# Selective scan in a two-layer block: carried states copied by ScalarE in every batch; in the first batch, two directions added to y by TensorE and a quarter of GpSimd's C products made by VectorE

## The chip, the cores and the metric

The kernel runs on one core of one Trainium2 chip. Its engines work on instruction streams of their own, each in order, and wait for each other by semaphores: TensorE (PE, with its weight loads as PEld), VectorE (DVE), ScalarE (ACT), GpSimd (POOL) and SyncE (SP), which issues most of the DMAs. The metric is the device time of one execution in microseconds. Before the change it is 4207.36 us, the median of three runs (4205.96 to 4208.89).

## The reference, cut to what matters

The input x has shape (4, 384, 32, 32), all in float32. Two layers follow each other, each with a mixer and a feed-forward part; the change lies in the first layer's mixer, a selective scan over the image in four directions:

```python
xs = _cross_scan(x)      # rows, columns, and both of these backwards: (B, 4, 384, 1024)
x_dbl = jnp.einsum('bkdl,kcd->bkcl', xs, x_proj_weight)
dts, Bs, Cs = (x_dbl[:, :, :R], x_dbl[:, :, R:R + N], x_dbl[:, :, R + N:])
dt = jax.nn.softplus(einsum(dts, dt_projs_weight) + dt_projs_bias)
def step(h, inp):        # over the 1024 positions, with 16 states n per channel d
    dA = jnp.exp(dtt[..., None] * A)
    h = h * dA + (dtt * ut)[..., None] * bt[:, :, None, :]
    y = jnp.einsum('bkdn,bkn->bkd', h, ct)
ys = ys + Ds * u         # then the four directions are turned back and added to y
```

After it come a layer norm with GELU and a residual, an expert layer (two of four experts per token), and in the second layer an attention with 8 heads and a factored feed-forward.

## The kernel before, in words

**Stages.** `scan_layer` runs the scan of the four batches one after the other. When a batch's scan is done, `between` puts the rest of the work of the batch before it (routing, experts, attention, feed-forward) into the program, so that the tail of batch b runs beside the scan of batch b + 1. The tail of the last batch stands alone at the end.

**The scan's units.** A unit is (batch, direction k, half i of the sequence), 512 positions long; the directions come in `ORDER = (0, 1, 3, 2)`, so k = 2 is the last. A unit has three chunks of 128 channels (`chunk`), and a chunk four state groups g of four states. In a group, partitions hold 4 states x 32 channels, and the chunk's 128 channels are four blocks j of 32, in two pairs q. For each pair:

- POOL multiplies `dtr` (dt times u, spread over the states by DMA) by the B rows `bcs` into `bx`, 128x1024 (L445);
- ACT makes `da`, the exponential of dt times A, into PSUM, 128x512 for each block (L454); `da` has two buffers;
- DVE scans each block (L459). In pair 0 the states go into `bx` in SBUF, in pair 1 into `da` in PSUM. In the first half of a sequence the scan starts from zero, in the second half from `carry`;
- in pair 1, DVE copies the last column of the state into `carry` in the first half (L465), and multiplies the state by the C rows into `bx` (L466);
- in pair 0, DVE copies two last columns in the first half (L470), and POOL multiplies both blocks of `bx` by the C rows, 128x1024 (L473);
- PE sums over the states with `sel`, into the chunk's `acc` in PSUM (L480).

`bx` has six buffers; `acc` shares two banks of PSUM with the other products of the scan (`dt_ps`, `xd_ps`, the layer norms). After a chunk, DVE adds `acc` into `y`: with D times u at k = 0 (L291), else L295. For k = 1 and 3, `y` is read and written by columns of the image. `project` makes dt, dt times u and the B and C rows of the next unit while a unit runs. In batch 0 its softplus is summed by PE with identity products (L383) and needs no POOL; in the other batches POOL and DVE do it (L400, L401, L407).

**What sets the order.** The program is written in the order above, but a scheduler that simulates a timeline puts the instructions of each engine into the order in which they then stand in that engine's stream. `place_behind` asks that parts of `project` stand behind the current group's POOL and DVE products. On the chip each stream is in order: an instruction that waits holds everything behind it on its engine.

Of the kernel before, what the change touches and what calls it, by code (L numbers as in the profile page):

```python
# [17 lines left out]
P = 128  # L18
# [5 lines left out]
HF = 512  # L24
# [3 lines left out]
ORDER = (0, 1, 3, 2)  # L28
# [30 lines left out]
NG = NS // NJ  # L59
# [54 lines left out]
def halves(i):  # L114
    return slice(i * HF, (i + 1) * HF)


class Body:
# [69 lines left out]
    def scan_layer(self, x1, between):  # L188

        nc, tc, a = self.nc, self.tc, self.a  # L190
        with ExitStack() as ctx:
# [23 lines left out]
            def start(b):  # L215
                x = work.tile([P, DC, L], F32, tag="u", name="u")
                src = a["x"][b].rearrange("(c p) l -> p c l", p=P)
                if b > 0:
                    nc.sync.dma_start(out=x, in_=src)
                    self.layernorm(x, x, self.eps6, psum, work)  # L220
                    return x

                for i in range(NH):
                    nc.sync.dma_start(out=x[:, :, halves(i)], in_=src[:, :, halves(i)])
                self.layernorm(x, x, self.eps6, psum, work, parts=[0])
                return x

            def finish(b, y, i):

                self.layernorm(y, y, self.eps5, psum, work, parts=[i])  # L230
                for c in range(DC):
                    ins = nc.scalar.activation(
                        y[:, c, halves(i)], y[:, c, halves(i)], AF.Gelu,
                        bias=self.col("lnb", c), scale=self.col("lnw", c),
                    ).ins
                    rows = slice(c * P, (c + 1) * P)
                    x = work.tile([P, HF], F32, tag="k2", name="x", bufs=6)
                    nc.sync.dma_start(out=x, in_=a["x"][b][rows, halves(i)])
                    nc.gpsimd.tensor_add(x, x, y[:, c, halves(i)])
                    if i == 0 and b < B - 1:  # L240
                        self.fresh.setdefault(b, []).append(x)
                    else:
                        nc.sync.dma_start(out=x1[b][rows, halves(i)], in_=x)
                self.exp_again(ins)
# [17 lines left out]
            carry = None  # L262
            for n, unit in enumerate(units):
                b, k, i = unit
                fed, ahead = ahead, []
                project = iter(())
                if n + 1 < len(units):
                    nb = units[n + 1][0]
                    if nb not in us:
                        us[nb] = start(nb)  # L270
                    project = self.project(units[n + 1], us[nb], wx, work, dram, psum, ahead)
                    next(project)
                if n % NH == 0:
                    carry = wp.tile([P, NB * NG], F32, tag=f"carry{n // NH % 2}", name="carry")
                if k == 0 and i == 0:
                    y = work.tile([P, DC, L], F32, tag="y", name="y")
                for c in range(DC):
                    acc = psum.tile([P, HF], F32, tag="ps", name="acc")
                    for _ in self.chunk(
                        unit, n % NH == 0, c, fed, carry, nega, sel, acc, work, dap  # L280
                    ):
                        next(project, None)
                    if k % 2 == 0:
                        ys = y[:, c, halves(i)]
                        out = acc
                    else:
                        w = slice(i * (HW // NH), (i + 1) * (HW // NH))
                        ys = y[:, c, :].rearrange("p (h w) -> p h w", h=HW)[:, :, w]
                        out = acc.rearrange("p (w h) -> p h w", h=HW)
                    if k == 0:  # L290
                        nc.vector.scalar_tensor_tensor(  # L291
                            ys, us[b][:, c, halves(i)], dsum[:, c : c + 1], out, op0=ALU.mult, op1=ALU.add
                        )
                    else:
                        nc.vector.tensor_add(ys, ys, out)  # L295
                if k == ORDER[-1]:
                    self.under_way.setdefault(b, fed[2])
                    finish(b, y, i)
                    if n + 1 == len(units) or units[n + 1][0] != b:
                        between(b)  # L300
# [113 lines left out]
    def chunk(self, unit, first, c, fed, carry, nega, sel, acc, work, dap):  # L414

        nc = self.nc
        b, k, i = unit
        bcs, dd, _ = fed  # L420
        dtr = []
        for q in range(NJ // 2):

            pair = []
            at = c * P + q * 2 * DB
            for s in range(2):
                t = work.tile([P, 2, HF], F32, tag="dtr", name="dtr", bufs=7)
                for n in range(NJ):
                    nc.sync.dma_start(
                        out=t[n * DB : (n + 1) * DB],  # L430
                        in_=dd[s, at : at + 2 * DB, :].rearrange("(j d) l -> d j l", d=DB),
                    )
                pair.append(t)
            dtr.append(pair)

        def run(ap):
            return ap[:, ::-1] if k >= 2 else ap

        last = 0 if k >= 2 else HF - 1
        for g in range(NG):  # L440
            bc = bcs[g]
            out = []
            for q in range(NJ // 2):
                bx = work.tile([P, 2, HF], F32, tag="bx", name="bx", bufs=6)
                pool = nc.gpsimd.tensor_mul(  # L445
                    bx, dtr[q][1], bc[:, 0].unsqueeze(1).to_broadcast([P, 2, HF])
                ).ins
                cg = bc[:, 1]
                at = ((c * 2 + q) * NG + g) * 2
                for j in range(2):  # L450
                    block = c * NJ + 2 * q + j
                    col = (k * NB + block) * NG + g
                    da = dap.tile([P, HF], F32, tag="da", name="da")
                    nc.scalar.activation(  # L454
                        da, dtr[q][0][:, j, :], AF.Exp, scale=nega[:, col : col + 1]
                    )
                    hold = carry[:, at + j : at + j + 1]
                    h = bx[:, j, :] if q == 0 else da
                    nc.vector.tensor_tensor_scan(  # L459
                        run(h), run(da), run(bx[:, j, :]), 0.0 if first else hold,  # L460
                        ALU.mult, ALU.add,
                    )
                    if q == 1:
                        if first:
                            nc.vector.tensor_copy(hold, h[:, last : last + 1])  # L465
                        dve = nc.vector.tensor_mul(bx[:, j, :], h, cg).ins  # L466
                if q == 0:
                    if first:
                        for j in range(2):
                            nc.vector.tensor_copy(  # L470
                                carry[:, at + j : at + j + 1], bx[:, j, last : last + 1]
                            )
                    pool = nc.gpsimd.tensor_mul(  # L473
                        bx, bx, cg.unsqueeze(1).to_broadcast([P, 2, HF])
                    ).ins
                out.append(bx)
            for q in range(NJ // 2):
                for j in range(2):
                    lo = (2 * q + j) * DB
                    nc.tensor.matmul(  # L480
                        acc[lo : lo + DB, :], sel, out[q][:, j, :],
                        start=(g == 0), stop=(g == NG - 1),
                    )
            self.place_behind = {"pool": pool, "dve": dve}
            yield
# [1087 lines left out]
```

## Time and profile before

| | before |
|---|---|
| median of three runs | 4207.36 us |
| the profiled execution | 4218.98 us, span 4217.2 us |
| scan of batch 0 (first to last scan instruction) | 44.0 to 748.6 us |
| scan of batches 1, 2, 3 | 751.9 to 1641.7, 1650.8 to 2541.5, 2542.2 to 3423.0 us |
| busy: PE, DVE, ACT, POOL | 3343.3, 2870.7, 2505.8, 3020.9 us |
| L445, POOL | 768 times 2359 ns |
| L473, POOL | 384 times 2360 ns |
| L459, DVE | 1536 scans of 1210 to 1273 ns |
| L466, DVE | 768 times 679 ns |
| L465 and L470, DVE | 384 times 149 ns and 384 times 142 ns |
| L454, ACT | 1536 times 690 ns |
| L295, DVE | 72 times 678 ns |

How to read it: the profile is one execution, taken by the hardware's profiler. A line such as "L473 POOL TENSOR_TENSOR bx<-bx,bcs" is a group of instructions by source line, engine, operation, and names of what is written and read. In a timeline, a line has the start, the time taken, the engine, the line, and in brackets how long the engine had been idle and what ended that. In the page's slices each digit is the busy share of one fortieth of the span, in tenths. A program's float32 product on PE shows as two matmul records.

### The profile page before, as it was taken

The numbers are of one execution on the slowest core, as the hardware profiler recorded it, in microseconds if no ns is written. First come the engines' busy times: TensorE is split into PE (matmuls) and PEld (weight loads), VectorE is DVE, ScalarE is ACT, GpSimd is POOL, SyncE is SP. The second block draws the span as 40 slices with busy tenths as digits, with TensorE's granted clock in tenths as the row PEclk, the third lists the DMA queues.
The fourth block names the chain that finished last, engine by engine and source line by source line (L and its number), as shares of the span: only waits on it lengthen the run. The fifth ranks groups of instructions, "written<-read, shape, count | busy, mean of one in ns | idle before, by whom it ended". The sixth has DMA issues, their size and how long they took to land. (4 is left out here: it accounts for less than half of the span.)

```text
span 4217.2 us, 45878 instructions
## 1 busy us (share of the span) xinstructions
PE 3343.3 (79%) x13372; PEld 1576.0 (37%) x13372; DVE 2870.7 (68%) x4250; ACT 2505.8 (59%) x4510; POOL 3020.9 (72%) x1476
## 2 busy tenths in 40 slices
PE   6445544389987888699987888789986898999899
PEld 2111111155653223255553223246553234676333
DVE  5999997878887777788877877788887851100101
ACT  5555555466665776766665775766665763533353
POOL 5999997888989877889989976988989941000100
PEclk9666666589998999799998998789998999999999
DMA  5454464577886444578886434578886424446200
GB/s 144 126 130 124 124 172 107 163 221 219 250 245 171 110 121 126 169 227 227 238 245 184 125 94 133 163 212 228 243 252 188 109 71 154 129 169 217 64 6 31
DMA packets 378882, 677.65 MB, mean 161 GB/s; under 512 B 49920, under 2 KB 179328, under 8 KB 378624
## 3 DMA queue, kind: packets, MB, share of 16 engines
q1 hardware_dynamic: 368800, 647.42, 54.0%
q0 software_dynamic: 8192, 25.21, 2.0%
q8 instruction: 107, 1.75, 0.2%
q10 hardware_dynamic: 1632, 2.04, 0.2%
q14 instruction: 151, 1.24, 0.1%
HBM read 566.68 MB, written 107.79 MB: 160 GB/s over the span
## 5 line engine op out<-in xcount | busy, mean ns | idle before, releaser
L445 POOL TENSOR_TENSOR bx<-dtr,bcs 128x1024 f32<-128x1024 f32 x768 | 1792.6, 2359 | 181.7 <-PE acc L480 99.5
L454 ACT ACTIVATE da<-dtr,nega 128x512 f32<-128x512 f32 x1536 | 1044.7, 690 | 920.4 <-DVE bx L466 568.7
L473 POOL TENSOR_TENSOR bx<-bx,bcs 128x1024 f32<-128x1024 f32 x384 | 904.5, 2360 | 139.7 <-DVE carry L470 68.2
L480 PE MATMUL acc<-bx,sel 128*32 128x512 f32 x3072 | 491.0, 700 | 322.5 <-POOL bx L473 296.2
L990 PE MATMUL h_ps<-xc,w 128*128 128x256 f32 (+1 forms) x3168 | 652.1, 361 | 55.4 <-DMA w<-in_w 31.7
L1011 PE MATMUL y_ps<-w,hs 128*128 128x384 f32 x1824 | 634.9, 501 | 34.2 <-ACT hs L1003 23.0
L990 PEld LDWEIGHTS h_ps<-xc,w 128*128 128x128 f32 x3168 | 546.2, 195 | 210.5 <-issue 94.6
L459 DVE TENSOR_TENSOR_SCAN bx<-da,carry,bx 128x512 f32<-128x512 f32 x384 | 474.0, 1269 | 116.3 <-POOL bx L445 61.2
L459 DVE TENSOR_TENSOR_SCAN da<-da,carry,bx 128x512 f32<-128x512 f32 x384 | 475.8, 1273 | 74.5 <-ACT da L454 67.1
L459 DVE TENSOR_TENSOR_SCAN bx<-da,bx 128x512 f32<-128x512 f32 x384 | 451.8, 1210 | 98.4 <-POOL bx L445 55.7
L466 DVE TENSOR_TENSOR bx<-da,bcs 128x512 f32<-128x512 f32 x768 | 509.0, 679 | 3.9 <-DMA bcs<-both 0.4
L459 DVE TENSOR_TENSOR_SCAN da<-da,bx 128x512 f32<-128x512 f32 x384 | 455.2, 1218 | 69.0 <-ACT da L454 55.8
L1011 PEld LDWEIGHTS y_ps<-w,hs 128*128 128x128 f32 x1824 | 348.7, 195 | 317.9 <-issue 60.8
L1144 PE MATMUL s_ps<-w 64*128 64x512 f32 x1024 | 310.3, 663 | 75.4 <-ACT ex L1150 71.4
L1150 ACT ACTIVATE ex<-s_ps 128x512 f32<-128x512 f32 x512 | 300.5, 591 | 107.6 <-PE s_ps L1144 106.2
L1042 POOL DMA_INDIRECT got<-made,g_source x64 | 61.0, 954 | 422.4 <-DMA made<-y 402.7
L998 ACT ACTIVATE hs<-h_ps,bb 128x256 f32<-128x256 f32 (+1 forms) x528 | 200.0, 440 | 230.2 <-PE h_ps L990 229.8
L1193 PE MATMUL o_acc<-ex,vt 128*64 128x512 f32 x1024 | 286.9, 637 | 24.4 <-ACT ex L1150 21.0
L480 PEld LDWEIGHTS acc<-bx,sel 128*32 128x32 f32 x3072 | 73.4, 115 | 610.5 <-POOL bx L473 403.1
L1015 DVE TENSOR_TENSOR y<-y_ps,bb 128x384 f32<-128x384 f32 x76 | 41.7, 548 | 255.9 <-PE y_ps L1011 255.9
L1144 PEld LDWEIGHTS s_ps<-w 64*128 64x128 f32 x1024 | 83.6, 191 | 285.4 <-ACT ex L1150 238.1
L370 PE MATMUL dt_ps<-xd,wdt 108*128 108x512 f32 x192 | 121.9, 721 | 58.8 <-ACT mag L409 29.3
(240 smaller groups left out, 3630.4 us busy)
## 6 DMA issues: line engine op xcount, KB each, us to landing
w<-in_w SPq DMA_DIRECT2D x352, 576.0 KB
dtr<-dd SPq DMA_DIRECT2D x1536, 128.0 KB
bcs<-both SPq DMA_DIRECT2D x512, 128.0 KB
dd<-one_e SPq DMA_DIRECT2D x96, 256.0 KB
dd<-mag SPq DMA_DIRECT2D x96, 256.0 KB
xt<-x SPq DMA_DIRECT2D x32, 384.0 KB
made<-y SPq DMA_DIRECT2D x32, 384.0 KB
xs<-rows SPq DMA_DIRECT2D x28, 385.0 KB
```

What stands on the lines that cost most here:

```text
L445: pool = nc.gpsimd.tensor_mul(bx, dtr[q][1], bc[:, 0].unsqueeze(1).to_broadcast([P, 2, HF])).ins
L454: nc.scalar.activation(da, dtr[q][0][:, j, :], AF.Exp, scale=nega[:, col : col + 1])
L459: nc.vector.tensor_tensor_scan(run(h), run(da), run(bx[:, j, :]), 0.0 if first else hold, ALU.mult, ALU.add,)
L466: dve = nc.vector.tensor_mul(bx[:, j, :], h, cg).ins
L473: pool = nc.gpsimd.tensor_mul(bx, bx, cg.unsqueeze(1).to_broadcast([P, 2, HF])).ins
L480: nc.tensor.matmul(acc[lo : lo + DB, :], sel, out[q][:, j, :], start=(g == 0), stop=(g == NG - 1),)
L990: ins = nc.tensor.matmul(ps[:, r, :], w1[(f + r) // wf][:, c, (f + r) % wf * P : ((f + r) % wf + 1) * P], xc[:, c, :], start=(c == 0), sto ...
L998: done = nc.scalar.activation(hs[:, f + r, :], ps[:, r, :], AF.Gelu if last else AF.Identity, bias=bb[:, f + r : f + r + 1],).ins
L1011: nc.tensor.matmul(out[:, :D], hs[:, f, t * P : (t + 1) * P], w2[f // wf][:, f % wf, :], start=(f == 0), stop=(f == FC - 1),)
L1144: ins = nc.tensor.matmul(ps, w[rows, j * P : (j + 1) * P], w[rows, halves(i)], start=True, stop=True).ins
L1150: done.append(nc.scalar.activation(ex[:, o, :], ps, AF.Exp, scale=HD**-0.5, accum_out=sums[:, t, 2 * j + o, i : i + 1],).ins)
L1193: ins = nc.tensor.matmul(out[cols, :], made[t][1][:, j, cols], ex[:, o, :], start=(j == 0), stop=(j == MB - 1),).ins
```

## The change

Three edits, all in the scan:

- The last column of a state goes into `carry` by a ScalarE copy instead of a VectorE copy, in every batch. For pair 0, one copy of two columns takes the place of two copies of one.
- In batch 0, for the directions 1 and 3, PE adds the chunk's part of `y` to `acc` by a product with the identity, which ends the accumulation, and ACT copies `acc` into `y`. Before, DVE added.
- In batch 0, in the groups 1 and 3, POOL multiplies one block of pair 0 by the C rows, 128x512, and DVE the other.

```diff
+                    if b == 0 and k not in (0, ORDER[-1]):
+                        nc.tensor.matmul(out, self.ident, ys, start=False, stop=True)
+                        nc.scalar.copy(ys, out)
-                    if k == 0:
+                    elif k == 0:
                         nc.vector.scalar_tensor_tensor(
                             ys, us[b][:, c, halves(i)], dsum[:, c : c + 1], out, op0=ALU.mult, op1=ALU.add
                         )
...
                     if q == 1:
                         if first:
-                            nc.vector.tensor_copy(hold, h[:, last : last + 1])
+                            nc.scalar.copy(hold, h[:, last : last + 1])
                         dve = nc.vector.tensor_mul(bx[:, j, :], h, cg).ins
                 if q == 0:
                     if first:
-                        for j in range(2):
-                            nc.vector.tensor_copy(
-                                carry[:, at + j : at + j + 1], bx[:, j, last : last + 1]
-                            )
-                    pool = nc.gpsimd.tensor_mul(
-                        bx, bx, cg.unsqueeze(1).to_broadcast([P, 2, HF])
-                    ).ins
+                        nc.scalar.copy(carry[:, at : at + 2], bx[:, :, last])
+                    if b == 0 and g % 2 == 1:
+                        pool = nc.gpsimd.tensor_mul(bx[:, 0, :], bx[:, 0, :], cg).ins
+                        nc.vector.tensor_mul(bx[:, 1, :], bx[:, 1, :], cg)
+                    else:
+                        pool = nc.gpsimd.tensor_mul(
+                            bx, bx, cg.unsqueeze(1).to_broadcast([P, 2, HF])
+                        ).ins
...
                         acc[lo : lo + DB, :], sel, out[q][:, j, :],
-                        start=(g == 0), stop=(g == NG - 1),
+                        start=(g == 0),
+                        stop=(g == NG - 1 and not (b == 0 and k not in (0, ORDER[-1]))),
```

## The prediction

> **What bounds the kernel now.** I read the page first (slices, groups), then the sums by stretch, then the timeline of the first batch, then single lines. In the chain that ended last, nothing of the scan stands: it is the last batch's attention and FFN on TensorE, the same instructions in both kernels. The change is therefore worth what it does to the stretch before that, the scan, which ends at about 3424 us. The slices on the page (about 105 us each) and the stretches:
>
> ```profile
> DVE  5999997878887777788877877788887851100101
> POOL 5999997888989877889989976988989941000100
> PEclk9666666589998999799998998789998999999999
> ...
> 133.70:634.20 500.50, 243.59 (x766) 59.43 (x766) 462.87 (x612) 266.81 (x416) 498.13 (x217) 0.65 0.53 134
> 634.20:751.90 117.70, 55.19 (x165) 18.08 (x165) 91.52 (x112) 62.33 (x97) 94.45 (x46) 0.63 0.43 114
> 751.90:1641.70 889.80, 723.84 (x3043) 356.88 (x3044) 711.04 (x1032) 579.45 (x1071) 768.93 (x376) 0.90 0.65 183
> ```
>
> The columns of the last three are the stretch, its length, busy time of PE, PE's weight loads, DVE, ACT and POOL, and the granted clock. The first is six half-sequences of batch 0: POOL is busy 498 of 500 us and DVE 463, while ACT and PE are about half idle. The third is batch 1, with the first batch's experts and attention beside the scan: nothing is full there (PE 81%, POOL 86%, DVE 80%, ACT 65%). So batch 0 is bound by POOL with DVE close behind, and batches 1 to 3 by the way the engines wait for each other. One state group of batch 0 in the timeline, DVE and then POOL:
>
> ```profile
> 308.47 2.46 DVE L459 TENSOR_TENSOR_SCAN bx<-da,carry,bx 128x512 f32<-128x512 f32 x2 [0.23 <-ACT da L454]
> 310.85 2.44 DVE L459 TENSOR_TENSOR_SCAN da<-da,carry,bx 128x512 f32<-128x512 f32 x2
> 313.20 1.26 DVE L466 TENSOR_TENSOR bx<-da,bcs 128x512 f32<-128x512 f32 x2
> 314.70 2.46 DVE L459 TENSOR_TENSOR_SCAN bx<-da,carry,bx 128x512 f32<-128x512 f32 x2 [0.23 <-ACT da L454]
> ...
> 311.05 4.64 POOL L445 TENSOR_TENSOR bx<-dtr,bcs 128x1024 f32<-128x1024 f32 x2
> 315.66 2.33 POOL L473 TENSOR_TENSOR bx<-bx,bcs 128x1024 f32<-128x1024 f32 x1
> 317.96 4.66 POOL L445 TENSOR_TENSOR bx<-dtr,bcs 128x1024 f32<-128x1024 f32 x2
> ```
>
> Starts, not durations, are what to read, since instructions of an engine overlap by 0.05 to 0.1 us. POOL goes round in 317.96 - 311.05 = 6.91 us; DVE could in 314.70 - 308.47 = 6.23 us, its 0.23 us wait for ACT within. Per chunk (four groups) POOL needs 27.7 us; measured are 500.5 / 18 = 27.8. DVE needs 4 x 6.23, the y add (0.60) and the product with u (0.83), 26.35 us. **The slack of DVE behind POOL is 1.4 us a chunk**; whatever is moved from POOL to DVE has to fit in it.
>
> **The change part by part.**
>
> *Carry copies (all batches).* DVE loses 384 copies at L465 and 384 at L470; ACT gets 384 and 192 (two columns in one). Their durations (149 and 142 ns) overstate what leaves DVE: in the timeline a copy of L465 moves the next start by 0.05 to 0.06 us, a pair of L470 by 0.20. The first half-sequence of each direction (the second has none) holds 24 and 12 of these, 24 x 0.055 + 12 x 0.20 = 3.7 us, or 1.2 a chunk. On ACT the nearest row is the 128x2 copy at L691, 0.18 us; 36 copies are 6.5 us a half-sequence. In ACT's order they stand between the exps: the copy from `bx` just ahead of the fourth exp of a group, the two from `da` ahead of the next group's first. Behind them wait the exps (and the scans on them), the dt chain, and in batches 1 to 3 the expert evictions L998 and the GELUs; POOL's C product now waits for ACT instead of DVE.
>
> *y adds of two directions (batch 0).* Twelve DVE adds (0.60 us) leave; PE gets twelve identity products (1.6 us each by the L383 rows, two passes of about 0.8), ACT twelve copies (0.585, row L409). PE is 49% and ACT 53% busy in batch 0, and the product stands behind the chunk's last sums, so I cost these at nothing; without that cover it is 12 x 2.2 = 26 us. DVE gains 0.3 a chunk over all.
>
> *A quarter of the C products (batch 0).* In 48 groups POOL's product halves: 2.31 becomes 1.22 (start to start of the 128x512 subtraction L400), 2.2 us less a chunk, 52 us in all. DVE gets 48 products of 0.60 us by L466. But L466 reads `da` in PSUM and one operand in SBUF; the new product reads `bx` and the C rows, both in SBUF, and no scan instruction of before does that. What such an instruction costs beside POOL, the few DVE lines with two SBUF inputs, and one with a tensor and a scalar column, show:
>
> ```profile
> 1607.48 1.55 DVE L1228 TENSOR_TENSOR wc<-wc,cols 128x384 f32<-128x384 f32 x1
> 2561.86 0.54 DVE L1228 TENSOR_TENSOR wc<-wc,cols 128x384 f32<-128x384 f32 x1
> ...
> 1607.36 1.26 POOL L400 TENSOR_TENSOR mag<-one_e,mag 128x512 f32<-128x512 f32 x1
> 1608.58 2.67 POOL L473 TENSOR_TENSOR bx<-bx,bcs 128x1024 f32<-128x1024 f32 x1
> ...
> 1250.85 1.27 DVE L970 TENSOR_TENSOR apart<-xs,full_i 128x8 f32<-128x8 f32 x1 [3.03 <-DMA xs<-rows]
> ...
> 2548.88 9.57 DVE L1223 TENSOR_SCALAR wb<-wb,c2mean 128x384 f32<-128x384 f32 x1 [4.17 <-DMA wb<-in_wb]
> ...
> 2548.95 9.28 POOL L445 TENSOR_TENSOR bx<-dtr,bcs 128x1024 f32<-128x1024 f32 x4
> ```
>
> The same product takes 0.54 us with POOL idle and 1.55 while POOL works: it ended 0.4 us after the POOL instruction that was running, and POOL's next took 2.67 instead of 2.36. L970 took 1.27 and 0.27 beside POOL against 0.17 without. So DVE waits for the running POOL instruction: 1.0, 1.1 and 0.1 us, mean 0.73; POOL loses up to 0.31. The L1223 row, another kind, waited through four POOL instructions.
>
> The Trainium skill (SBUF — State Buffer, Who interferes with whom) says this against the change: a VectorE instruction with two SBUF inputs takes a read port that GpSimd needs too, and the later of the two blocks until the first has finished. By that rule a product that meets a 2.3 us instruction at a random moment would wait an estimated 1.15 us, 55 us for 48. The rows here say 0.73, or 35 us; the 9.57 row shows more than the one instruction that the page allows.
>
> *Batch 0, sum.* POOL: 27.7 - 2.2 + 2 x 0.31 = 26.1 us a chunk; it is no longer the bound. DVE, bare: 26.35 + 2 x 0.60 - 0.3 (y) - 0.6 (copies, 1.2 in every second half-sequence) = 26.65, or 24 x (26.65 - 27.8) = -28 us: the low end. With 2 x 0.73 of port waits it is 28.1. DVE also waited, between 100 and 630 us, 8.8 us for the second pair's exps and 4.2 for the dt product, 0.7 a chunk, which POOL's pace hid and DVE's does not; part of it falls together with the port waits, so I take half: 28.45, **+16 us**. High end: 2 x 1.1 and all of the 0.7, 29.55, +42 us. What is late next is DVE; POOL will idle at its C products.
>
> *Batches 1 to 3, sum.* Twelve first half-sequences: 12 x 3.7 = 44 us leave DVE, 12 x 6.5 = 78 us come to ACT. Both wait for each other there: between 752 and 3424 us ACT waits 584 us for DVE before its exps, DVE 190 us for these exps. With ACT's waits the larger I take three quarters of the copies as hidden (+20) and count 0.35 of what DVE loses (-15): **+5 us**, between -30 (two thirds of DVE's share, copies hidden) and +50 (two thirds of ACT's on the path).
>
> *Rest.* No DMA is added or taken away. By the built program's order the experts and attention stand beside the same chunks as before, mostly within a twelfth of a half-sequence (the latest, attention of batch 1, a quarter later), so I give the order nothing. Sum: +21 us. The profiled execution took 4219.0 us (span 4217.2 and 1.8 around it), 11.6 above the median of 4207.4; it would go to 4240, the median to 4228.
>
> **The rivals.**
>
> *Faster: the products meet POOL while it waits.* If DVE is the bound, POOL runs ahead and stands idle at its half product, which needs the same scan as DVE's half; DVE then starts first and waits for nothing. For it: the two halves are ready together. Against it: after a C product POOL has two L445 (4.6 us) and arrives at the next about when DVE does. It gives -28 us in batch 0, and with 0 to -5 beyond about 4177. It decides if the wait per product is under 0.2 to 0.4 us: bare DVE is 1.15 a chunk below now, less the 0.35 to 0.7 of other waits, for two products.
>
> *Slower still, by ScalarE.* The copies wait in order for scans, and evictions and GELUs (L1003, 2.77 us with two table loads of 1.28) behind them start late. For it: DVE's largest wait in batches 1 to 3 is for ACT (112 us for the second pair). +50 there with +16 in batch 0 give 4273.
>
> *No difference.* POOL's 52 us leave the bound and the port waits eat just that: about 4207. Here too belongs that a stage does what the change says (POOL falls to some 94%) and the end does not move.
>
> **How the numbers follow.** A measurement here can tell about 0.2%, 8.4 us, from no change. Forecast (port waits of about 0.7): 0.46, its own range 4212 to 4255. ScalarE on the path: 0.12. No difference: 0.14. Faster: 0.28. Slower is 0.46 + 0.12 = 0.58. The range goes from 4172 (the faster case and 5 us) to 4275 (the ScalarE case, or waits of 1.1 with some +20 beyond); below and above it I leave 0.08 each.
>
> **What would show it.** Right: the new VectorE product has a mean well above 0.68 us, near 1.4, and those over 1 us end just behind a POOL instruction; POOL is under 97% busy in batch 0 and waits for DVE's scans at the C products; a chunk of batch 0 takes 28 us or more. Right for ScalarE: the small copies take about 0.18 us and the exps after them start no later. Wrong: the product's mean is 0.7 and a chunk takes 27 us or less (faster), or batches 1 to 3 (890, 900 and 882 us now) change by more than 15 us each, which nothing in my sum carries.

## The result, and the profile after

The changed kernel takes 4285.21 us (median of five runs, 4277.44 to 4289.87), the kernel before took 4208.89 us beside it (4205.96 to 4214.97). The ratio is 1.0175, with an interval of 1.0159 to 1.0191: slower by some 76 us. The forecast was 4228 us, with a range up to 4275. The direction was right, the size less than a third of what came, and the time lies outside the range.

The profiled execution after took 4289.86 us, with a span of 4288.0 us: 70.8 us more span than before. Read by the first and last scan instruction of each batch, these divide as follows.

| stretch | before | after | difference | forecast |
|---|---|---|---|---|
| first scan of batch 0 to first scan of batch 1 | 707.9 | 746.8 | +38.9 | +16 |
| from there to the last scan of batch 3 | 2671.1 | 2692.1 | +21.0 | +5 |
| from there to the end | 794.2 | 804.8 | +10.6 | 0 |

So half of the loss lies in batch 0, and nearly half behind it. The slices of the page after, in the rows that were shown of before:

```profile
DVE  6999998867887877687877877686887851000101
...
POOL 5988887888897978788988967888998941000100
PEclk8777766579998999789998999789998999999999
```

Of the five slices at 9 that POOL had at the start, one is left; DVE keeps its five. The stretches of the profile after (length, then busy time of PE, weight loads, DVE, ACT, POOL, and the granted clock). The first line is the whole of batch 0, the next two are its half-sequences 1 to 6 and the last one, the fourth is batch 1, the fifth batches 1 to 3:

```profile
44.30:791.10 746.80, 404.42 (x1099) 106.26 (x1097) 678.07 (x700) 398.24 (x743) 644.78 (x298) 0.72 0.48 124
...
137.10:675.10 538.00, 295.78 (x792) 73.55 (x791) 495.63 (x492) 283.76 (x536) 475.82 (x218) 0.72 0.50 127
675.10:791.10 116.00, 54.27 (x160) 17.68 (x157) 97.59 (x118) 62.55 (x96) 88.28 (x45) 0.63 0.39 106
791.10:1691.40 900.30, 723.74 (x3054) 356.65 (x3055) 703.68 (x841) 591.38 (x1215) 768.19 (x375) 0.90 0.64 182
...
791.10:3483.20 2692.10, 2233.43 (x9291) 1092.50 (x9291) 2104.18 (x2555) 1814.01 (x3612) 2301.34 (x1123) 0.91 0.64 182
```

And the whole of batch 0, and batches 1 to 3, in the kernel before:

```profile
44.00:751.90 707.90, 350.57 (x1076) 92.29 (x1074) 635.53 (x856) 377.30 (x588) 674.67 (x297) 0.67 0.51 131
...
751.90:3423.00 2671.10, 2234.18 (x9299) 1091.74 (x9299) 2135.26 (x3130) 1776.22 (x3185) 2303.10 (x1124) 0.91 0.65 184
```

Busy time and idle time are what to take from these. In batch 0 DVE's busy time grew from 635.5 to 678.1 us, by 42.6; its idle time went from 72.4 to 68.7 us, by -3.7. The two make the 38.9. POOL is busy 30 us less and idle 102 us where it was idle 33. So POOL did get its relief, and DVE got nothing for it: it waits as long as before, and works longer. In batches 1 to 3 the granted clock is 0.91 in both kernels and PE's busy time the same within 0.8 us (2234.2 and 2233.4), so a slower TensorE is not what lengthens them.

What the new instructions cost (groups of the profile after: busy time, mean ns of one, then the engine's idle time ahead and what ended it):

```profile
L477 POOL TENSOR_TENSOR bx<-bx,bcs 128x1024 f32<-128x1024 f32 x336 | 793.8, 2366 | 194.1 <-ACT carry L472 95.4 <-DVE bx L462 92.7 <-DMA bcs<-both 3.7
...
L469 DVE TENSOR_TENSOR bx<-da,bcs 128x512 f32<-128x512 f32 x768 | 497.8, 677 | 48.8 <-ACT carry L468 45.5 <-DMA dtr<-dd 0.3
...
L475 DVE TENSOR_TENSOR bx<-bx,bcs 128x512 f32<-128x512 f32 x48 | 68.6, 1429 | 5.4 <-ACT carry L472 4.7
L474 POOL TENSOR_TENSOR bx<-bx,bcs 128x512 f32<-128x512 f32 x48 | 68.2, 1420 | 17.8 <-ACT carry L472 12.2 <-DVE bx L462 5.6
```

L475 is the new VectorE product, with 1.43 us in the mean where the product from PSUM (L469) takes 0.68. L469 stands here for another reason, which was not foreseen: it now waits 45.5 us for ScalarE's copy of the carry. Both read the same tile `da`, and the built program makes the second reader wait for the first.

A stretch of batch 0 in the timeline after, DVE and then POOL (start, time taken, and in brackets the wait before):

```profile
321.35 2.46 DVE L462 TENSOR_TENSOR_SCAN bx<-da,carry,bx 128x512 f32<-128x512 f32 x2 [1.31 <-POOL bx L448]
323.85 2.63 DVE L475 TENSOR_TENSOR bx<-bx,bcs 128x512 f32<-128x512 f32 x1
326.40 2.45 DVE L462 TENSOR_TENSOR_SCAN da<-da,carry,bx 128x512 f32<-128x512 f32 x2
...
338.98 0.69 DVE L475 TENSOR_TENSOR bx<-bx,bcs 128x512 f32<-128x512 f32 x1
...
316.65 2.34 POOL L477 TENSOR_TENSOR bx<-bx,bcs 128x1024 f32<-128x1024 f32 x1 [0.53 <-DVE bx L462]
318.95 14.35 POOL L448 TENSOR_TENSOR bx<-dtr,bcs 128x1024 f32<-128x1024 f32 x6
333.27 1.25 POOL L474 TENSOR_TENSOR bx<-bx,bcs 128x512 f32<-128x512 f32 x1
```

The first product stands at 323.85 us, in the middle of six POOL instructions of 2.39 us that run from 318.95 on; the third ends at 325.93 and the product 0.55 us behind it, at 326.48. So do all 30 of the 48 products that take over 1 us: each ends 0.55 us behind the end of a POOL instruction. The second one meets the end of a POOL instruction and takes 0.69 us.

### The profile page after: what moved, and what is told of

The parts are those of the page before. It is cut to its first block, busy times and chain, and to the rows that moved or that the text cites. A ratio compares the mean times of both kernels' runs of the same rounds, so it can differ in the third digit from the quotient of the medians.

```text
span 4288.0 us, 45952 instructions
## 1 busy us (share of the span) xinstructions
PE 3400.4 (79%) x13396; PEld 1590.3 (37%) x13396; DVE 2882.8 (67%) x3518; ACT 2564.7 (60%) x5094; POOL 2989.2 (70%) x1476
## 5 line engine op out<-in xcount | busy, mean ns | idle before, releaser
L477 POOL TENSOR_TENSOR bx<-bx,bcs 128x1024 f32<-128x1024 f32 x336 | 793.8, 2366 | 194.1 <-ACT carry L472 95.4
L484 PE MATMUL acc<-bx,sel 128*32 128x512 f32 x3072 | 540.3, 710 | 272.5 <-POOL bx L477 181.3
L995 PE MATMUL h_ps<-xc,w 128*128 128x256 f32 (+1 forms) x3168 | 661.0, 364 | 71.2 <-DMA w<-in_w 45.1
L469 DVE TENSOR_TENSOR bx<-da,bcs 128x512 f32<-128x512 f32 x768 | 497.8, 677 | 48.8 <-ACT carry L468 45.5
L1149 PE MATMUL s_ps<-w 64*128 64x512 f32 x1024 | 305.6, 661 | 72.1 <-ACT ex L1155 64.9
L484 PEld LDWEIGHTS acc<-bx,sel 128*32 128x32 f32 x3072 | 84.1, 117 | 597.3 <-POOL bx L477 243.3
L468 ACT COPY carry<-da 128x1 f32<-128x1 f32 x384 | 60.4, 162 | 203.2 <-DVE da L462 200.5
```

The costliest lines, as they stand in the source:

```text
L477: pool = nc.gpsimd.tensor_mul(bx, bx, cg.unsqueeze(1).to_broadcast([P, 2, HF])).ins
L484: nc.tensor.matmul(acc[lo : lo + DB, :], sel, out[q][:, j, :], start=(g == 0), stop=(g == NG - 1 and not (b == 0 and k not in (0, ORDER[-1 ...
L995: ins = nc.tensor.matmul(ps[:, r, :], w1[(f + r) // wf][:, c, (f + r) % wf * P : ((f + r) % wf + 1) * P], xc[:, c, :], start=(c == 0), sto ...
L1149: ins = nc.tensor.matmul(ps, w[rows, j * P : (j + 1) * P], w[rows, halves(i)], start=True, stop=True).ins
```

## The experiments

The two theories at the start: A, ScalarE's copies make the loss; B, the C products on VectorE make it. All times "behind batch 0" below are from the first scan of batch 1 to the end of the execution, "batch 0" is from first scan to first scan, both from the profile. The medians of the kernel before differ by up to 0.6% from chip to chip (4208.9 to 4233.2 us), so ratios are given, each with its interval, against the kernel before on the same chip. The stretches come from one profiled execution of each kernel, all set beside the one profile of the kernel before; where that was another chip, the ratio is the surer number. Worked out from the ratio, less batch 0's own difference, the loss behind batch 0 lies between 18 us below and 7 us above the one by the profiles (25 for 42 us in the last row), but keeps its sign wherever it is over 10 us.

| kernel | ratio | batch 0 | of it DVE idle | behind batch 0 |
|---|---|---|---|---|
| before | 1 | 707.9 | 72.4 | 3465.3 |
| the change | 1.0175 [1.0159, 1.0191] | 746.8 | 68.7 | 3496.9 |
| carry copies alone | 0.9978 [0.9962, 0.9994] | 705.6 | 85.7 | 3453.2 |
| y adds alone | 1.0003 [0.9988, 1.0018] | 704.6 | 76.2 | 3467.8 |
| C products alone | 1.0261 [1.0239, 1.0282] | 746.1 | 42.2 | 3536.5 |
| all but the carry copies | 1.0259 [1.0228, 1.0289] | 739.0 | 44.4 | 3542.1 |
| all but the C products | 0.9982 [0.9967, 0.9996] | 703.3 | 90.8 | 3467.4 |
| C products alone, from PSUM | 1.0126 [1.0109, 1.0143] | 710.1 | 41.1 | 3509.7 |
| the change, C products from PSUM | 1.0068 [1.0044, 1.0091] | 711.1 | 64.9 | 3507.6 |

**One part alone, and one part left out.** The edits are those of the change's diff, taken singly. Carry copies alone:

> Only the carry copies move to ScalarE, in every batch; the y adds and the C products stay as before. Theory A (the copies in ScalarE's line): VectorE's product behind a scan and GpSimd's C product wait for a copy that stands behind other ScalarE work; in the changed kernel VectorE waits 44 us for the copy from da and GpSimd 71 us for the copy from bx after the first batch, so this alone costs 30 to 60 us: 4237 to 4267. Theory B (the shared port): the copies have no part in the loss, 4200 to 4215.

Y adds alone:

> Only the y adds of directions 1 and 3 of batch 0 move to TensorE and ScalarE. Both theories: GpSimd still bounds batch 0, so 4200 to 4212; a gain of at most 8 us by 12 VectorE adds of 0.6 us. If TensorE's product or ScalarE's copy stood on the path it would be up to 26 us slower.

C products alone:

> Only the quarter of the C products moves to VectorE, in batch 0. Theory B (the shared port): the new product has a mean near 1.4 us; with the copies still on VectorE a chunk of batch 0 takes 26.35 + 1.2 + 1.5 = 29.0 us and more, +25 to +45 us: 4232 to 4252. Theory A: under +10 us, 4200 to 4217.

All but the carry copies:

> The changed kernel with the carry copies put back on VectorE. Theory A: most of the 76 us goes, 4207 to 4235, and batches 1 to 3 take what they took before (890, 891 and 881 us). Theory B: batch 0 stays as long as in the changed kernel (744 us) or longer, 4245 and more.

Measured: 0.9978, 1.0003, 1.0261, 1.0259. Theory A falls: the carry copies alone make the kernel 0.2% faster. Theory B is right in kind, but the products alone cost 112 us of span, far more than B had foreseen, and more than the whole change. All but 3 of the 112 us lie in two places, 38 in batch 0 and 71 behind it, where the program asks for the same work as before. These two are taken apart below.

**What the products cost in batch 0.** The block that VectorE multiplies is scanned into `da` in PSUM, so that the product reads one operand from SBUF and no longer two:

```diff
+                    own = q == 0 and j == 1 and b == 0 and g % 2 == 1
-                    h = bx[:, j, :] if q == 0 else da
+                    h = bx[:, j, :] if q == 0 and not own else da
...
+                    if own:
...
+                        nc.vector.tensor_mul(bx[:, j, :], h, cg)
...
```

> The kernel before, with the C product of one block of pair 0 made by VectorE in the groups 1 and 3 of batch 0, as in the change, but the block's states are scanned into da in PSUM, so the product on VectorE reads only one operand from SBUF. Theory P (the price of batch 0 is the product's wait beside GpSimd): the product takes 0.67 to 0.8 us and no longer 1.48 us, which is 33 to 39 us less on VectorE, and GpSimd's half product 1.25 to 1.30 us; batch 0 takes 700 to 718 us (704.6 before, 743.6 with the product from SBUF). Rival Q (it is the order of the waits between VectorE, GpSimd and the loads, whatever the product takes): batch 0 takes 730 to 745 us. For batches 1 to 3 (2671 us from the first scan of batch 1 to the last of batch 3 before, 2746 us with the product from SBUF): theory O (their time goes by the order that the scheduler gave them, which this kernel changes too) says more than 15 us off 2671 us, to either side; rival L (they pay for a late batch 0, whose rest work runs beside them) says 2661 to 2681 us where batch 0 comes out under 718 us.

The same with the whole change:

> The whole change, with the block that VectorE multiplies in batch 0 scanned into da in PSUM, so that the product reads one operand from SBUF alone. Theory P (the product's wait beside GpSimd is the price of batch 0): 695 to 712 us for batch 0 where the change has 744.4, the product 0.67 to 0.8 us. Theory Q (the chunk is held by the other waits): 730 to 745 us. With batches 1 to 3 and the rest behind them between the 3465 us of before and the 3510 us of the run with the product alone from PSUM: 4205 to 4265 us in all.

The product's group and POOL's half product in the second of these:

```profile
L480 POOL TENSOR_TENSOR bx<-bx,bcs 128x512 f32<-128x512 f32 x48 | 60.8, 1266 | 4.7 <-DVE bx L463 2.9 <-ACT carry L478 1.7
...
L470 DVE TENSOR_TENSOR bx<-da,bcs 128x512 f32<-128x512 f32 x48 | 32.9, 685 | 3.5 <-ACT carry L469 2.8
```

0.685 us and none over 0.69; POOL's half 1.27 instead of 1.42. Batch 0 falls by 36.0 us (746.1 to 710.1) and by 35.7 us (746.8 to 711.1). The products' excess over 0.685 us was 38.2 and 35.7 us in 48 instructions. DVE's idle time hardly moves (42.2 to 41.1, 68.7 to 64.9 us). **The wait of the products beside POOL lies on the path, almost microsecond for microsecond.** Theory P is shown, Q falls.

Two more doses came from other placings of the same products: the blocks exchanged (DVE takes block 0), and the groups 0 and 2 for 1 and 3.

```diff
-                        pool = nc.gpsimd.tensor_mul(bx[:, 0, :], bx[:, 0, :], cg).ins
-                        nc.vector.tensor_mul(bx[:, 1, :], bx[:, 1, :], cg)
+                        pool = nc.gpsimd.tensor_mul(bx[:, 1, :], bx[:, 1, :], cg).ins
+                        nc.vector.tensor_mul(bx[:, 0, :], bx[:, 0, :], cg)
```

> The C products of batch 0 alone, in the same groups 1 and 3, with the two blocks exchanged: VectorE multiplies block 0 and GpSimd block 1. The work of every batch is that of the run with VectorE on block 1; the written order of batches 1 to 3 is another. Price of the product in batch 0: 735 to 755 us (743.6 with block 1). Theory O (the loss of batches 1 to 3 goes by the order): from the first scan of batch 1 to the last of batch 3, 15 us or more away from the 2746 us of block 1; it cannot say where between 2650 and 2760 us. Rival S (something else in the program with the C products, the same whatever the order): 2736 to 2756 us.

> The C products of batch 0 alone, in the groups 0 and 2 and no longer 1 and 3. The same 48 products on VectorE. Price in batch 0 as before: 735 to 755 us. Batches 1 to 3, by theory O 15 us or more away from 2746 us; by rival S 2736 to 2756 us.

The product's group with the blocks exchanged:

```profile
L475 DVE TENSOR_TENSOR bx<-bx,bcs 128x512 f32<-128x512 f32 x48 | 97.1, 2023 | 0.7
```

Batch 0 missed the expected 735 to 755 us in both: 782.8 and 766.9 from first scan to first scan (781.4 and 765.5 to its last scan). The product took 2.02 and 1.79 us in the mean, so its excess was 64.2 and 52.9 us, and batch 0 is 72.7 and 56.8 us longer than with the product from PSUM. The wait depends on what POOL is doing when the product arrives, and the price follows it. Batches 1 to 3 took 2706.8 and 2729.5 us, 39 and 16 us less than with the products alone as the change places them: as theory O has it, the first clearly and the second barely, and outside rival S's 2736 to 2756 us. In ratio: 1.0260 [1.0218, 1.0303] and 1.0280 [1.0242, 1.0317].

**The carry copies in batch 0.** The table's DVE idle column tells what they do there. With the C products and the copies on VectorE, DVE's idle time falls from 72.4 to 41 to 44 us: the slack is recovered. With the copies on ScalarE it is 65 to 69 us. All but the carry copies, in batch 0:

```profile
44.30:783.30 739.00, 416.59 (x1098) 108.50 (x1097) 694.56 (x891) 381.49 (x599) 644.60 (x298) 0.70 0.48 125
```

Against the change, DVE works 694.6 us for 678.1 there, so the copies on ScalarE take 16.5 us from DVE; and they add 24.3 us of idle time. What ended the waits in batch 0 of that kernel, for POOL and DVE (us in total, times, longest):

```profile
POOL bx L477 <- DVE carry L473: 11.9, 9, 2.0
...
POOL bx L480 <- DVE carry L473: 9.2, 8, 4.8
...
DVE bx L462 <- POOL bx L448: 4.3, 4, 2.8
DVE da L462 <- POOL bx L448: 2.0, 1, 2.0
```

and in batch 0 of the change:

```profile
POOL bx L477 <- ACT carry L472: 24.5, 6, 6.7
...
POOL bx L474 <- ACT carry L472: 12.2, 7, 2.9
...
DVE bx L462 <- POOL bx L448: 18.7, 14, 2.5
...
DVE da L462 <- POOL bx L448: 6.7, 3, 2.8
```

POOL's waits for the carry at its C products go from 21.1 to 36.7 us, and DVE's waits for POOL's products with the B rows, which stand behind these in POOL's order, from 6.3 to 25.4. The written order of batch 0 differs between the two kernels as well (by source line and operand names, 60 per cent of POOL's instructions there stand in the same sequence), so this pair does not part the copies' waits from the order that came with them. The pair with the products from PSUM (41.1 and 64.9 us of idle time) shows the same size, but differs in its order too, and by the y adds.

**The copy behind the product.** To take away L469's wait for ScalarE, the copy out of `da` is put behind the product in the program of the carry copies alone:

```diff
-                        if first:
-                            nc.scalar.copy(hold, h[:, last : last + 1])
                         dve = nc.vector.tensor_mul(bx[:, j, :], h, cg).ins
+                        if first:
+                            nc.scalar.copy(hold, h[:, last : last + 1])
```

> The carry copies on ScalarE in all batches, as in the change, but the copy out of da stands behind VectorE's C product of the same block in the program, so that VectorE's product no longer waits for ScalarE's copy of the same tile; ScalarE's copy waits for the product. Theory W (in the change VectorE's waits for ScalarE's copies, 44 us in batches 1 to 3, lie on the path): 4165 to 4195 us beside 4205.6 us with the copies in the change's order. Rival N (ScalarE's copy now holds the next exponential instead, or these waits lie beside others): 4200 to 4225 us.

Measured 1.0053 [1.0036, 1.0070], 4238.09 us, beyond both ranges. ScalarE's copy out of `da` with the carry copies alone, and in this run:

```profile
L465 ACT COPY carry<-da 128x1 f32<-128x1 f32 x384 | 60.1, 162 | 193.4 <-DVE da L459 190.0 <-DVE places L781 1.0
...
L466 ACT COPY carry<-da 128x1 f32<-128x1 f32 x384 | 60.5, 159 | 274.2 <-DVE bx L464 272.9
```

VectorE's wait is gone. ScalarE waits 274 us at these copies, but it had waited 193 us there already, and ahead of the exps it now waits 572.7 us for 661.6: with the two-column copies, its idle time at these three groups is 907 us in the one run and 908 in the other. So nothing came of the wait that was taken away, and theory W finds no support. The written order behind batch 0 is another as well (55 per cent of VectorE's instructions stand in the same sequence); where the 33 us against the copies in the change's order come from was not told apart.

**What is lost behind batch 0.** Theory O: the scheduler, whose picture of batch 0 the change alters, writes another order for everything behind it, and this order costs. Rival L: batches 1 to 3 pay for a late batch 0. The run with the products from PSUM speaks against L: batch 0 ends 2 us late, and 44 us are lost behind it. Next, the same perturbation of the program with no work moved: POOL makes both halves itself.

```diff
-                    pool = nc.gpsimd.tensor_mul(
-                        bx, bx, cg.unsqueeze(1).to_broadcast([P, 2, HF])
-                    ).ins
+                    if b == 0 and g % 2 == 1:
+                        nc.gpsimd.tensor_mul(bx[:, 1, :], bx[:, 1, :], cg)
+                        pool = nc.gpsimd.tensor_mul(bx[:, 0, :], bx[:, 0, :], cg).ins
...
```

> The kernel before, with no work moved: in the groups 1 and 3 of batch 0 GpSimd makes both halves of the product itself, in two instructions of 128x512 for one of 128x1024. GpSimd's work grows by 48 times (2 x 1.26 - 2.36) us = 8 us in batch 0, VectorE's and ScalarE's work is the same. The order that the scheduler writes for batches 1 to 3 changes about as much as with the change's products. Theory O (order alone): batches 1 to 3 together take 2671 us plus or minus more than 15 us. Rival L (batches 1 to 3 lose because batch 0 ends late): 2661 to 2681 us together, since batch 0 is at most 10 us longer. Batch 0 by both: 704 to 715 us.

Batch 0 took 718.7 us (704 to 715 expected), and behind it 3452.3 us, 13 less than before; ratio 1.0001 [0.9988, 1.0015]. Batches 1 to 3 alone moved by -12 us: too little for O's 15, so inconclusive. Then the products in batch 3 in place of batch 0 (`b == 3` in the change's condition):

> The kernel before with the change's C products on VectorE in the groups 1 and 3 of batch 3, and no longer of batch 0. The written order of batches 0 and 1 is nearly that of before, that of batches 2 and 3 is another. Theory O (the loss of batches 1 to 3 came with their order, not with a property of the program): batches 0 and 1 are within 5 us of before (704.6 and 889.8 us); batch 3 pays for its own products 15 to 55 us (880.8 us before), by the product's wait beside GpSimd, 24 to 48 us in 48 products, less what GpSimd gets back; ratio 1.003 to 1.015. If the place in batch 0 does not matter and the whole 112 us belong to the 48 products, the ratio is 1.02 to 1.03 again.

Batches 0 and 1 came back as before (704.2 and 892.1 us), and batch 2 too (891.5); batch 3 took 921.7 for 880.8, and the rest 809.8 for 794.2. Ratio 1.0134 [1.0114, 1.0154]. So the products cost 41 us where they stand, and ahead of them, where the order is that of before, nothing is lost. The rest is 16 us longer because more of the work was left for it: PE is busy 751.9 us there for 732.9.

The whole change with the blocks exchanged:

> The whole change, with the blocks exchanged between VectorE and GpSimd in the 48 products. Batch 0 as in the change, 735 to 755 us (744.4). Batches 1 to 3 with the change take 2692 us from the first scan of batch 1 to the last of batch 3, the rest behind them 805 us. Theory O: the sum of the two, 3497 us, moves by 10 us or more to either side, though no work differs. Rival S: 3487 to 3507 us.

1.0160 [1.0121, 1.0200]; batch 0 755.7 us, at the edge of its range, and behind it 3492.0 us, 5 off: inconclusive for O. Up to here, by the profiles, every kernel with the products in batch 0 had lost 27 to 77 us behind it; those without them stood between -13 and +3 there, but for the 22 us with the copy behind the product. The decisive kernels change the order with batch 0 left as it is: a single C product of batch 1 is written as two POOL instructions.

```diff
+                    if (b, k, i, c, g) == (1, 1, 0, 0, 0):
+                        nc.gpsimd.tensor_mul(bx[:, 0, :], bx[:, 0, :], cg)
+                        pool = nc.gpsimd.tensor_mul(bx[:, 1, :], bx[:, 1, :], cg).ins
+                    else:
...
```

In the first direction of batch 1, `(1, 0, 0, 0, 0)`:

> The kernel before, all its work on its engines, except that one single C product in the first group of batch 1 is written as two GpSimd instructions of 128x512 for one of 128x1024: 0.2 us of work. Batch 0 stays as it was (704.6 us); the scheduler writes another order from there on. From the first scan of batch 1 to the end, before: 3465 us. Theory O (the order alone makes the losses of 32 to 77 us seen there): off by more than 10 us, and in one of the two kernels of this kind 3490 us or more. Rival S2 (these losses need the products on VectorE in batch 0; without them the order moves it by -13 to +3 us, as in the runs so far): 3450 to 3470 us.

In the second direction:

> As the one before, with the one product split in the second direction of batch 1. Theory O: off 3465 us by more than 10 us, in one of the two 3490 us or more; rival S2: 3450 to 3470 us.

With the products alone:

> The C products of batch 0 alone on VectorE in the groups 1 and 3, and the one product of batch 1 written as two GpSimd instructions. Batch 0 as without the split, 738 to 750 us (743.6). From the first scan of batch 1 to the end: 3536 us without the split. Theory O: 15 us or more away from it, likelier below; S2: 3510 to 3545 us.

With the whole change:

> The whole change, and the one product of batch 1 written as two GpSimd instructions. Batch 0 744 us as with the change, plus or minus 5. From the first scan of batch 1 to the end 3497 us with the change: theory O 10 us or more away from it, S2 3487 to 3507 us.

| kernel with one product split | ratio | batch 0 | behind batch 0 | without the split |
|---|---|---|---|---|
| before, first direction | 1.0019 [1.0006, 1.0033] | 707.3 | 3474.8 | 3465.3 |
| before, second direction | 1.0075 [1.0051, 1.0098] | 707.9 | 3497.8 | 3465.3 |
| C products alone | 1.0170 [1.0139, 1.0201] | 746.4 | 3516.0 | 3536.5 |
| the change | 1.0143 [1.0114, 1.0172] | 743.6 | 3494.5 | 3496.9 |

Batches 1 to 3 of the kernel before with the split in the second direction (the line before has 2671.10 us):

```profile
754.30:3454.40 2700.10, 2227.68 (x9287) 1092.08 (x9287) 2148.79 (x3130) 1795.01 (x3191) 2304.15 (x1126) 0.90 0.63 182
```

A product split in two, 0.2 us of work, in a program whose batch 0 is untouched, costs 32.5 us: 29.0 in batches 1 to 3, where POOL's busy time is the same within 1.1 us. Single half-sequences move more: the first of batch 2 takes 168.0 us for 146.4. And the split gives 20.5 of the 71 us back that the products alone had lost (some 38 by the ratios). **An order of its own, without any product on VectorE, makes a loss as large as that of the change behind batch 0**, as theory O had it for one of the two kernels without products; S2's 3450 to 3470 us is missed by both. The first direction (9.5 us off) and the whole change (2.4 off) fell short of the 10 us that O had asked for, and tell nothing by themselves.

One price of an order can be counted. ScalarE's stream holds table loads (ACT_TABLE_LOAD, 1.283 us each in these traces), and how many there are goes by the order: 141 in the kernel before, 154 with the second split, 157 with the C products alone, 139 when these have the split. That is 16.7 and 20.5 us more of ScalarE's time in the two orders that lose 32.5 and 71 us. But it is not what the change pays: the change has 137 loads, four fewer than before, as have both kernels with products from PSUM.

Last, the same order in two kernels. All but the C products has, behind batch 0, nearly the order of the carry copies alone:

> The change without its C products: carry copies on ScalarE, and the y adds of two directions in batch 0 on TensorE and ScalarE. Its written order behind batch 0 is nearly that of the carry copies alone (VectorE's and GpSimd's streams agree to 93 to 98 per cent there). Theory O, now in the other direction (the same order gives the same time): from the first scan of batch 1 to the end 3453 us, as with the carry copies alone, plus or minus 8; batch 0 698 to 704 us; ratio 0.995 to 0.999. If the order is not what sets these batches, no such agreement is expected, and the range of the runs so far holds, 3450 to 3500 us.

3467.4 us for 3453.2: 14 off, more than the 8 that were expected; the ratios, each on its own chip, are 0.9982 and 0.9978. By source line and operand names, VectorE, GpSimd and ScalarE have the same sequence of instructions behind batch 0 in both traces (between before and the second split 39, 61 and 50 per cent stand in the same sequence). The half-sequences 8 to 31 of the two, counted from 0 through all batches, agree to 4.0 us each but one (147.9 for 141.3), also where both differ from before by over 10 us: half-sequence 12 takes 133.2 and 132.6, before 119.5. Other pairs with one sequence behind batch 0 stand as close: before and the y adds alone 2.5 us, C products alone and all but the carry copies 5.6. Differences under about 20 us behind batch 0 are therefore not read.

This bears on the change itself. Behind batch 0 it has the same instructions as the carry copies alone, but for four table loads fewer; only their sequence differs (39 per cent of VectorE's stand as there). Yet it takes 3496.9 us there for 3453.2 and 3467.4. The work is the same, and a late batch 0 does not explain it, since with the products from PSUM batch 0 is 36 us shorter, and what lies behind it moves by 11 us at most. That leaves the order.

What stays open is which place in these orders costs. The largest change of a wait, with the C products alone, from the first scan of batch 1 to the last of batch 3, is that of POOL for buffers that PE's sums have not yet read:

```profile
POOL bx L445 <- PE acc L484: 144.8, 33, 20.1
POOL mag L400 <- ACT one_e L387: 65.8, 16, 9.1
```

Before, the first was 88.4 us and the second 34.8. But in the kernel before with the second split, which loses 32.5 us, the first is 91.3 us, and in the change it is 75.4. No one wait, and no count of table loads, carries the loss in all of them. Nor is it excluded that the products' presence in the scheduler's picture tends towards bad orders: with products on VectorE in batch 0, every order that ran lost between 27 and 77 us behind it; without them, and with the copies as before, it went from -13 to +32.5.

## Why the prediction was wrong, point by point

*The price of the product: right.* "The rows here say 0.73, or 35 us": 48 products waited 35.7 us, with a mean of 1.43 us for the expected "near 1.4". Those over 1 us end behind a POOL instruction, as the timeline shows. That the hit is so close is partly luck: it came from three rows of other instructions, and in the other runs the same products waited between 0.70 and 1.34 us each. POOL's share, "up to 0.31 us" each, was a little more: its busy time in batch 0 is 18.6 us higher than in the change with the products from PSUM (644.8 for 626.2), 0.39 us each. The page's rule (the Trainium skill, SBUF — State Buffer, Who interferes with whom) says too that a VectorE instruction with at most one SBUF input, outside its two-port modes, does not contend with GpSimd; the 0.685 us of the product from PSUM agree.

*DVE's work in batch 0: right.* From 26.35 to 26.65 us and 2 x 0.73 a chunk make 1.76, or 42 us in 24 chunks; measured 42.6.

*DVE's idle time in batch 0: wrong, and the first step that failed.* The sum set 26.65 against the 27.8 of now, and so counted "the slack of DVE behind POOL", 1.4 us a chunk, as recovered, but for "half" of 0.7: about -26 us of idle time. Measured are -3.7. The slack can be recovered: with the copies left on VectorE the idle time falls by 28.0 us. It was the term "- 0.6 (copies)" that failed, which counted what leaves DVE and put the waits that come in its place at nothing. The text had said that "POOL's C product now waits for ACT instead of DVE", and priced it for batches 1 to 3 alone. In batch 0 the copies on ScalarE, with the order that came with them, take 16.5 us from DVE and give 24.3 back in waits; they cost 7.8 where -14 were counted, and these 22 us are nearly all of what lies between +16 and +39.

*The y adds: right.* Alone 1.0003, and batch 0 is 3.3 us shorter.

*Batches 1 to 3 by the copies: right in size.* Expected +5, between -30 and +50; alone they make -12 us behind batch 0, and +2 together with the y adds. "ScalarE on the path" (4273) would have been close in time, but in batches 1 to 3, where it put its 50 us, the copies alone do not cost them.

*"I give the order nothing": wrong, and the second step that failed.* It rested on the experts and attention standing "beside the same chunks as before, mostly within a twelfth of a half-sequence". Where the instructions stand does not tell what an order costs: a single split product moves the time behind batch 0 by 32.5 us, nearly half the loss of the change, with batch 0 as before and 13 table loads of ScalarE more. In the change it was 31.6 us, with +5 expected: 27 us, which with the 23 of batch 0 make the 50 us between the forecast +21 and the 70.8 of the profiles. That an order can cost this much is shown. That it does so in the change follows from the same instructions taking 30 to 44 us less in another order; which waits in it cost, and whether they are those at the copies, stays open.

*Of the rivals*, "faster" needed waits under 0.2 to 0.4 us a product; with the product from PSUM, where the wait is zero, batch 0 still takes 711 us against 707.9, so the rival's 28 us did not come even then. With the copies on VectorE, DVE's idle time is then 41.1 us, but its busy time has grown by 33.5, which takes the gain.

*The signs.* A chunk took 29.9 us (538.0 / 18) for 28 or more, POOL was 88% busy (475.8 of 538.0) for under 97, as said; the small copies took 0.16 and 0.19 us for "about 0.18". "Or batches 1 to 3 change by more than 15 us each" was named as a sign of error: they changed by 10.5, 15.2 and 2.8 us, and the rest by 10.6.

## What to carry to other kernels

Before work goes from GpSimd to VectorE, look where its operands lie: two in SBUF meant 0.74 us of waiting for each product, nearly all of it on the path, one in PSUM meant none. When a small copy moves to another engine, price the wait of every instruction that needs its tile, also in the stage where that engine is half idle: here, in an order of its own, it gave back more than it took. And where a scheduler writes the order, changing a stage re-writes all stages behind it: compare a harmless change of the same program first, since here that alone moved the time by up to 0.75%.

## What was unexpected of the hardware

A product with two SBUF operands can wait for more than one GpSimd instruction. In batch 3 (the run with the products there) one took 9.53 us. DVE, and below it POOL, at that place of the timeline:

```profile
3282.82 9.53 DVE L475 TENSOR_TENSOR bx<-bx,bcs 128x512 f32<-128x512 f32 x1
```

```profile
3277.77 11.59 POOL L445 TENSOR_TENSOR bx<-dtr,bcs 128x1024 f32<-128x1024 f32 x5
3289.32 1.25 POOL L474 TENSOR_TENSOR bx<-bx,bcs 128x512 f32<-128x512 f32 x1
3290.55 1.25 POOL L400 TENSOR_TENSOR mag<-one_e,mag 128x512 f32<-128x512 f32 x1
```

POOL ran without a gap from 3277.77 to 3291.8, and the product ended at 3292.35, 0.55 us behind the last of them; then POOL stood idle. The next longest took 7.93 us and ended likewise, behind the last POOL instruction before an idle stretch. In batch 0 none took over 2.9, and the one at 323.85 us shown above came through after one POOL instruction though six stood in a row. The Trainium skill (SBUF — State Buffer, SBUF: two separate sides) says that the later of the two blocks for the other's whole instruction; this row, like the 9.57 us row that the prediction showed, goes beyond one instruction, and no run here shows what decides it.
